# A decoder layer on one core: normalized tokens exchanged through HBM, two buffers for the feed-forward's rows, weights fetched in another order

## The chip, the cores and the metric

The kernel runs on one core of a Trainium2 chip. The metric is the time on the device in microseconds (us), the median of several executions. A profiled execution gives the trace from which all rows below are taken. The engines are TensorE (PE, with its weight loads as PEld), VectorE (DVE), ScalarE (ACT), GpSimd (POOL) and SyncE (SP); a "q" behind an engine's name (SPq) means its instruction queue, here the issuing of DMAs.

## The reference

All numbers are float32. The input `x` is [4, 1024, 512]: four batches of 1024 tokens of 512 features. `_layernorm` has no scale and no shift. Cut to what matters:

```python
def attn(x):              # x is normalized; 16 heads of 32
    aperture, expression = sigmoid(x @ Wa + ba), sigmoid(x @ We + be)   # one number per token and head
    inner, outer, v = x @ Wi, x @ Wo, x @ Wv
    w = softmax(inner @ outer.T / sqrt(32)) * aperture[q] * expression[k]
    w = w / (w.sum(-1) + 1e-8)
    converged = w @ v
    # per head: scale by sigmoid(iv), rotate the two halves of the 32 features, scale by sigmoid(ov), tanh(chi)
    return rotated @ Wout

def xattn(query, key_value):   # key_value is [4, 1024, 384]; 16 heads of 32
    q, k, v = query @ Wq + bq, key_value @ Wk + bk, key_value @ Wv + bv
    return softmax(clip(q @ k.T * 32 ** -0.5)) @ v @ Wo + bo

def ffn(x):                    # 64 units, each with 16 inner values of its own
    s = x @ Win + bin_
    h = relu(s[..., None] * W1 + b1)
    g = einsum('btmh,mh->btm', h, W2) + b2
    return g @ Wout + bout

x = x + attn(_layernorm(x))
x = x + xattn(_layernorm(x), ctx)
x = x + ffn(_layernorm(x))
```

## The kernel before

**Units and halves.** The work is cut in eight units: the gated self-attention of each of the four batches (phase 0, units 0 to 3), then the cross-attention of each (phase 1, units 4 to 7). The feed-forward follows the cross-attention of its tokens. A unit has two halves `hf` of 512 queries. The attention of a half runs over four groups `g` of four heads and, in each, over eight tiles `kt` of 128 keys: 32 steps. In a step, PE computes the scores `s` (L537), ScalarE takes two exponentials `e` of [128, 1024] (L542), VectorE adds them to the running sum `es` (L548, L550; in phase 0 also the gated sum, L558), and one step later PE multiplies `e` by the values into `av` (L564). At the end of a group the sums over partitions are taken with `ones` on PE (L594), they go to HBM and come back as [128, 16] to be inverted, and the reciprocals `rec` return to divide the result (`q`, L644).

**What lies beside the attention.** Everything else is cut into small parts with a cost each, and `run` puts parts between the steps of an attention. The list `beside(u, hf)` gives their order: the projections of the next unit (queries `q`, keys `k`, values `v`, gates `g` and `gt`, layer norm `ln` and transposes `tr`) and the `post` of the half that has just ended (output projection `o`, residual, layer norm, and in phase 1 the feed-forward). What has to be done before the first attention is written out in a list called `first`. `weave` interleaves two lists.

**Order on the engines.** PE, VectorE, ScalarE and GpSimd keep the order in which the program issues instructions (`manual_schedule`). SP and the DMAs are placed by the scheduler; nearly all large DMAs are issued by SP, whose queue is in order: an issue that has to wait for a buffer or for data holds up those behind it.

**Exchange of partitions.** Matmuls need the features on the partitions. `normalized` (L287) writes normalized tokens with tokens on partitions; 32-by-32 blocks are turned by VectorE's `blocks` (L296), and what remains is to exchange blocks between partitions. For the input of an attention, `spread` (L289 to L293) does this with sixteen DMAs of 64 KB from SBUF to SBUF: `xT<-xin`. For the feed-forward, each of four normalized tiles of 128 tokens goes into a tile `r2` (shown as `r` in the profile) of a pool with one buffer, and from there into `rows_d` in HBM (L729, 256 KB each); after the fourth, four DMAs bring it back in the exchanged order into `xn` (L732). The matmul of the feed-forward's first layer is L747.

**The feed-forward's middle.** A half has `s` for two groups of units on 128 partitions. For each of the 16 inner values `h`, ScalarE computes a tile `hid` (L762) from a pool of three buffers, and VectorE adds it, weighted, to `g` (L766, L768). The parts are woven between the steps of the attention. The last matmul of the feed-forward is L779.

**Weights.** `load_w` fetches a weight of 1 MB (or 768 KB) into a pool of three buffers. Four of the weights are fetched by `by_quarters`, L92, in an order of rows that fits the blocks. The weight `Wout` of the self-attention is loaded once (`load_wout`, L151), turned on PE by the heads' rotations (`rotations`, `rotate`), and written to HBM as `wout_d` (L188), from which it is fetched for every use. In the self-attention the weight of the keys is named `Wo`, that of the queries `Wi`.

Of the kernel before, what the change touches and what calls it, by code (L numbers as in the profile page):

```python
# [16 lines left out]
P = 128  # L17
# [22 lines left out]
NB = 32  # L40
# [23 lines left out]
def moderate_path(tc: tile.TileContext, a: dict, out: bass.AP, flag: bass.AP):  # L64
    nc = tc.nc
    x = a["x"]
    with ExitStack() as st:
# [20 lines left out]

        def by_quarters(dma, to, w):

            for q in range(NC):
                dma(to[ts(q, NB)], w[ts(q, P)].rearrange("(c i) f -> i c f", i=NB))  # L92

        x1_d = [[dram.tile([P, D], F32, tag=f"mx1_{b}_{t}", name="x1_d") for t in range(NT)] for b in range(B)]
        x1b_d = [[dram.tile([P, D], F32, tag=f"mxb_{b}_{t}", name="x1b_d") for t in range(NT)] for b in range(B)]
# [2 lines left out]
        sum1_d = [dram.tile([HG, HALF], F32, tag=f"sum1_{i}", name="sum1_d") for i in range(4)]  # L98
        sum2_d = [dram.tile([2, HG, HALF], F32, tag=f"sum2_{i}", name="sum2_d") for i in range(4)]
        rec_d = [dram.tile([HG, HALF], F32, tag=f"rec_{i}", name="rec_d") for i in range(4)]  # L100
        rows_d = [dram.tile([4, P, D], F32, tag=f"rows_{i}", name="rows_d") for i in range(2)]
        wout_d = dram.tile([P, NC, D], F32, name="wout_d")

        ident = const.tile([P, P], F32, name="ident")
# [47 lines left out]
            nc.sync.dma_start(rotj, a["rotj"])  # L152
            nc.sync.dma_start(hp, a["headp"])

        rot = p1.tile([P, NC, P], F32, tag="r2", name="rot")

        def rotations():

# [127 lines left out]
        def normalized(to, xt, mv, rs, i):  # L286
            nc.vector.tensor_scalar(to, xt, mv[:, i, 0:1], rs[:, i : i + 1], ALU.subtract, ALU.mult)  # L287

        def spread(to, xt):  # L289

            for q in range(NC):
                for s in range(P // NB):
                    nc.sync.dma_start(to[ts(q, NB), :, ts(s, P)], xt[ts(s, NB), :, ts(q, P)])  # L293

        def blocks(xt, t):
            nc.vector.transpose(xt[:, t, :], xt[:, t, :])  # L296
# [33 lines left out]
        def pre(u):  # L330
# [29 lines left out]
            def ln(hf):  # L360
                res = {}

                def stats(t):
                    def f():
                        if t == 0:
                            res["mv"] = p2.tile([P, 4, 2], F32, tag="bnmv", name="bnmv")
                        s6 = p2.tile([P, 6], F32, tag="bnst", name="bnst")
                        nc.vector.bn_stats(s6, me["xn", hf][:, t, :])  # L368
                        nc.vector.bn_aggr(res["mv"][:, t, :], s6)
                    return [(0, f)]  # L370

                def root():
                    res["rs"] = rsqrt(res["mv"], 4)

                def norm(t):
                    def f():
                        xt = me["xn", hf][:, t, :]
                        normalized(xt, xt, res["mv"], res["rs"], t)
                        if xt0(hf):
                            return  # L380
                        if t == 3:
                            me["xT", hf] = p2.tile([P, 4, D], F32, tag="inT", name="xT")
                            spread(me["xT", hf], me["xn", hf])
                    return [(0, f)]

                return [stats(t) for t in range(4)] + [[(0, root)]] + [norm(t) for t in range(4)]
# [4 lines left out]
            def tr(hf, t):  # L391
# [8 lines left out]
                    me["in", hf, "t"] = lambda c, i: chunk(xn, c, i, 1)  # L400
                return f

            def proj(what, g, hf):
                kind = "ctx" if ph == 1 and what == "k" else "in"
                n = NCK if kind == "ctx" else NC

                def part(cs):
                    def f():
                        if cs[0] == 0:
                            if g == 0 and hf == 0:  # L410
                                me["w" + what] = load_w(f"{what}{ph}")
                            me["pj"] = bank()
                        for c in cs:
                            columns(
                                me["pj"], me["w" + what][:, c, ts(g, P)], me[kind, hf](c),
                                start=(c == 0), stop=(c == n - 1),
                            )
                        if cs[-1] == n - 1:
                            copy(me["pj"])
                    return len(cs), f  # L420

                def copy(pj):
                    if what == "k":
                        if g == 0 and hf == 0:
                            me["k"] = p2.tile([P, NC, T], F32, tag="k", name="k")
                        dst = me["k"][:, g, ts(hf, HALF)]
                    else:
                        if g == 0:
                            me["q", hf] = p3.tile([P, NC, HALF], F32, tag="q", name="q")
                        dst = me["q", hf][:, g, :]  # L430
                    evacuate(dst, pj, bqk[:, 0 if what == "q" else 1, g : g + 1] if ph else None)

                return [part(list(range(0, 2))), part(list(range(2, n)))]
# [74 lines left out]
                return [[(load, f)]]  # L508

            vs = [values(kt) for kt in range(NT)]  # L510
            r = {"v": [vs[0:4], vs[4:8]]}
            for k, f, load in (
                ("ctx", load_ctx, 0), ("x", load_x, 0), ("g", gates, 1), ("gt", gates_t, 1),
            ):
# [153 lines left out]
        def post(u, hf):  # L668
# [18 lines left out]
            def project(t):  # L687
                def part(cs):
                    def f():
                        assert me["divided", hf] == HG - 1  # L690
                        if cs[0] == 0:
                            res["po"] = bank()
                        for c in cs:
                            columns(
                                res["po"], me["q", hf][:, c, ts(t, P)], me["wo"][:, c, :],
                                start=(c == 0), stop=(c == NC - 1),
                            )
                        if cs[-1] < NC - 1:
                            return
                        r = res[t]  # L700
                        nc.vector.tensor_tensor(r, res["po"], r, ALU.add)  # L701
                        if ph == 0:
                            nc.sync.dma_start(x1_d[b][4 * hf + t], r)
                            r2 = p1.tile([P, D], F32, tag="r2", name="r2")
                            nc.gpsimd.tensor_tensor(r2, r, bo_bc, ALU.add)  # L705
                            nc.sync.dma_start(x1b_d[b][4 * hf + t], r2)
                        else:
                            s6 = p2.tile([P, 6], F32, tag="bnst1", name="bnst1")
                            if t == 0:
                                res["mv"] = p2.tile([P, 4, 2], F32, tag="fmv", name="fmv")  # L710
                            nc.vector.bn_stats(s6, r)
                            nc.vector.bn_aggr(res["mv"][:, t, :], s6)
                    return len(cs), f
                return [part([0, 1]), part([2, 3])]
# [7 lines left out]
            def norm(t):  # L722
                def f():
                    if last:
                        normalized(res["xn"][:, t, :], res[t], res["mv"], res["rs"], t)
                    else:
                        r2 = p1.tile([P, D], F32, tag="r2", name="r2")
                        normalized(r2, res[t], res["mv"], res["rs"], t)
                        nc.sync.dma_start(rows_d[hf][t], r2)  # L729
                        if t == 3:  # L730
                            for q in range(NC):
                                nc.sync.dma_start(  # L732
                                    res["xn"][ts(q, NB)].rearrange("j t (s f) -> j (t s) f", f=P),
                                    rows_d[hf].rearrange("t (s j) f -> j (t s) f", j=NB)[:, :, ts(q, P)],
                                )
                    nc.gpsimd.tensor_tensor(res[t], res[t], bout_bc, ALU.add)
                return [(0, f)]

# [18 lines left out]
            def hidden(h):  # L757
                def f():

                    if h < INNER:  # L760
                        hid = p3.tile([P, 2 * P], F32, tag="hid", name="hid")
                        nc.scalar.activation(  # L762
                            hid, res["s"], AF.Relu, bias=units[:, 1, h : h + 1], scale=units[:, 0, h : h + 1]
                        )
# [72 lines left out]
        def beside(u, hf):  # L837
# [8 lines left out]
            if u + 1 < B:  # L846
                if hf == 0:
                    out = x[1] + k[0][0:1] + p["g"][0] + k[0][1:] + p["gt"][0]
                    if last:
                        out = last["load"] + out + weave(ln[1], last["o"])  # L850
                    else:
                        out = one(rotations) + one(fold_bv) + out + [rotate(c) for c in range(NC)] + ln[1]
                        out += [[(4, fold_bv)]]
                    return out + v[0][0:2] + tr[1] + v[0][2:3] + p["g"][1] + v[0][3:] + p["gt"][1]
                if not next_:
                    return k[1] + last["load"] + v[1] + last["o"] + q[0] + q[1]
# [20 lines left out]
        p = pres[0]  # L877
        first = p["x"][0] + p["ln"][0] + one(negate) + p["tr"][0] + p["k"][0] + p["x"][1] + p["g"][0]
        first += weave(p["ln"][1], p["q"][0]) + p["gt"][0] + p["v"][0][0:3] + p["tr"][1] + p["v"][0][3:] + p["k"][1]
        first += one(load_wout) + pres[1]["x"][0] + p["g"][1] + weave(pres[1]["ln"][0], p["q"][1]) + p["gt"][1]  # L880
        first += p["v"][1][0:3] + pres[1]["tr"][0] + p["v"][1][3:]
        run([lambda: None], first)
        for u in range(n):
            if u == 0:
# [664 lines left out]
```

## Time and profile before

| | us |
|---|---|
| median of three runs | 2363.6 (2359.71 to 2365.66) |
| profiled execution | 2356.22 |
| its span, first to last instruction | 2354.4 |
| PE busy | 2204.8 (94%) |
| VectorE busy | 1558.0 (66%) |
| ScalarE busy | 1231.3 (52%) |
| GpSimd busy | 139.8 (6%) |
| mean granted clock of TensorE | 0.973 |

163.08 MB move in 158343 DMA packets, 69 GB/s in the mean. The page cuts the span in 40 slices of 58.9 us and gives the busy share of each engine in tenths, and the clock that TensorE was granted, in tenths of full speed. Rows of the timeline have the start, the duration, the engine and its line, the operation, "output<-inputs" with shapes, how many instructions were merged, and in brackets how long the engine was idle before and what ended that.

### The profile page before, as it was taken

The page shows a single profiled execution, that of the slowest core. Times are in us where ns is not written, and L with a number is a line of the kernel's source. Part 1 is how long each engine was busy: PE and PEld are TensorE (multiplying, and loading weights), DVE is VectorE, ACT ScalarE, POOL GpSimd, SP SyncE. Part 2 cuts the span into 40 slices and gives each one's busy share as a digit, 9 for nine tenths or more (in the row PEclk, how much of TensorE's full clock was granted, in tenths as well). Part 3 has the DMA queues.
Part 4 walks back from the last instruction along what each step waited for, and adds up shares of the span by engine and source line. Part 5 has one row for each costly group of instructions (what it writes and reads, how often), then busy time and mean ns, then how long its engine had stood idle before and what let it go on. Part 6 is the DMA issues. An engine that isn't in the chain of part 4 may idle for free.

```text
span 2354.4 us, 53085 instructions
## 1 busy us (share of the span) xinstructions
PE 2204.8 (94%) x22610; PEld 555.1 (24%) x22610; DVE 1558.0 (66%) x2485; ACT 1231.3 (52%) x1478; POOL 139.8 (6%) x146
## 2 busy tenths in 40 slices
PE   7897999999999999999999997999899997999974
PEld 2221222222222222222222221222222221222211
DVE  4466666785767765666865677667886777745454
ACT  0053545555455544555556554647465663756551
POOL 3000012000000000000100001010000101010100
PEclk9998999999999999999999998999999998999997
DMA  5403122131321312112421223222322243212020
GB/s 121 131 8 96 31 83 73 36 107 26 101 63 39 93 45 78 51 39 74 117 72 39 83 78 91 74 61 82 104 59 66 78 118 82 65 31 58 29 65 25
DMA packets 158343, 163.08 MB, mean 69 GB/s; under 512 B 50560, under 2 KB 96256, under 8 KB 156944
## 3 DMA queue, kind: packets, MB, share of 16 engines
q1 hardware_dynamic: 154608, 158.55, 23.7%
q8 instruction: 179, 2.93, 0.5%
q0 software_dynamic: 2080, 0.98, 0.3%
q14 instruction: 68, 0.56, 0.1%
q10 hardware_dynamic: 1408, 0.07, 0.0%
HBM read 108.34 MB, written 35.42 MB: 61 GB/s over the span
## 4 chain that ended last, share of the span: by engine, by line
PE 78%; DVE 7%; DMA 7%; SPq 3%; issue 2%; ACT 1%; DVEq 0%; ACTq 0%
PE f L87 30%; PE s L537 21%; PE av L564 17%; PE sm L572 5%; SPq L293 2%; DMA rows_d<-r 2%; PE sm L594 2%; DVE es L550 2%; ACT e L542 1%; DMA xn<-rows_d 1%; PE f L747 1%; PE f L779 1%; DVE r L287 1%; DMA sum_d<-both 1%; DVE bnst L368 0%
## 5 line engine op out<-in xcount | busy, mean ns | idle before, releaser
L542 ACT ACTIVATE e<-s 128x1024 f32<-128x1024 f32 x1024 | 995.0, 1023 | 807.0 <-PE s L537 607.9
L550 DVE TENSOR_TENSOR es<-es,e 128x1024 f32<-128x1024 f32 x528 | 643.4, 1242 | 276.5 <-ACT e L542 275.6
L537 PE MATMUL s<-q,k 32*64 32x512 f32 x8192 | 619.0, 614 | 9.9 <-ACT e L542 8.7
L564 PE MATMUL av<-e,v 128*32 128x512 f32 x4096 | 556.4, 606 | 0.0
L87 PE MATMUL f<-xT,w 128*32 128x512 f32 x2816 | 334.5, 596 | 13.2 <-DMA w<-in_attn_Wo 8.8
L558 DVE SCALAR_TENSOR_TENSOR eg<-e,sw,eg 128x512 f32<-128x512 f32 x448 | 322.3, 754 | 2.3
L87 PE MATMUL f<-w,q 128*32 128x512 f32 x2048 | 246.0, 598 | 10.2 <-DVE q L644 10.2
L537 PEld LDWEIGHTS s<-q,k 32*64 32x64 f32 x8192 | 137.4, 130 | 461.9 <-ACT e L542 247.3
L548 DVE TENSOR_TENSOR es<-e 128x1024 f32<-128x1024 f32 x88 | 108.0, 1247 | 194.8 <-ACT e L542 186.9
L564 PEld LDWEIGHTS av<-e,v 128*32 128x32 f32 x4096 | 88.5, 108 | 405.8 <-issue 402.8
L87 PEld LDWEIGHTS f<-xT,w 128*32 128x32 f32 x2816 | 93.5, 111 | 228.1 <-issue 215.2
L572 PE MATMUL sm<-e,sw 128*2 128x512 f32 x1024 | 135.1, 599 | 0.0
L87 PE MATMUL f<-w,xT 128*32 128x512 f32 x896 | 106.3, 601 | 16.5 <-DMA w<-in_attn_Wv 16.0
L705 POOL TENSOR_TENSOR r<-res,bo_bc 128x512 f32<-128x512 f32 x32 | 46.5, 1452 | 1128.8 <-DVE res L701 1031.9
L594 PE MATMUL sm<-es,ones 128*1 128x512 f32 x352 | 74.0, 620 | 36.7 <-DVE es L550 36.0
L87 PEld LDWEIGHTS f<-w,q 128*32 128x32 f32 x2048 | 67.2, 111 | 166.7 <-issue 150.4
L762 ACT ACTIVATE hid<-sT,units 128x256 f32<-128x256 f32 x128 | 70.7, 612 | 59.9 <-DVE sT L753 58.0
L87 PE MATMUL f<-w,ctxT 128*32 128x512 f32 x768 | 92.8, 592 | 0.0
L87 PE MATMUL f<-ctxT,w 128*32 128x512 f32 x768 | 92.6, 592 | 0.0
L768 DVE SCALAR_TENSOR_TENSOR g<-hid,units,g 128x256 f32<-128x256 f32 x120 | 57.9, 482 | 21.2 <-ACT hid L762 13.3
L701 DVE TENSOR_TENSOR res<-f,res 128x512 f32<-128x512 f32 x64 | 43.9, 685 | 31.3 <-PE f L87 31.3
L644 DVE TENSOR_TENSOR q<-both,recb 128x512 f32<-128x512 f32 x64 | 44.6, 697 | 26.0 <-DMA recb<-rec_d 25.5
(238 smaller groups left out, 1058.2 us busy)
## 6 DMA issues: line engine op xcount, KB each, us to landing
recb<-rec_d SPq DMA_DIRECT2D x256, 64.0 KB
xT<-xin SPq DMA_DIRECT2D x240, 64.0 KB
w<-in_xattn_Wo SPq DMA_DIRECT2D x9, 1024.0 KB
xin<-in_x SPq DMA_DIRECT2D x8, 1024.0 KB
res<-in_x SPq DMA_DIRECT2D x32, 256.0 KB
w<-wout_d SPq DMA_DIRECT2D x8, 1024.0 KB
x_d<-res SPq DMA_DIRECT2D x32, 256.0 KB
x1b_d<-r SPq DMA_DIRECT2D x32, 256.0 KB
```

What stands on the lines that cost most here:

```text
L87: nc.tensor.matmul(to[r], lhsT=lhsT[:, j, :] if len(lhsT.shape) == 3 else lhsT[:, r], rhs=rhs, **flags)
L293: nc.sync.dma_start(to[ts(q, NB), :, ts(s, P)], xt[ts(s, NB), :, ts(q, P)])
L537: nc.tensor.matmul(s[m : m + 64, j, :], lhsT=k[r, g, kt * P + m : kt * P + m + 64], rhs=q[r, g, :], start=True, stop=True,)
L542: nc.scalar.activation(e, s, AF.Exp, scale=SCALE)
L548: nc.vector.tensor_tensor(me["es"][i], me["e", 0][i], es[i], ALU.add)
L550: nc.vector.tensor_tensor(me["es"][i], me["es"][i], es[i], ALU.add)
L558: nc.vector.scalar_tensor_tensor(eg, es[0][:, h, :], gate(kt), eg, ALU.mult, ALU.add)
L564: nc.tensor.matmul(av[r, :], lhsT=me["v"][:, kt, HG * g + h, :], rhs=es[h // 2][:, h % 2, :], start=(kt == 0), stop=(kt == NT - 1),)
L572: nc.tensor.matmul(sm[j * DH : j * DH + sums, :], lhsT=me["sw"][:, t, HG * g + 2 + h, :] if ph == 0 else ones, rhs=me["e", t][1][:, h, :], ...
L594: nc.tensor.matmul(sm[j * DH : j * DH + 1, :], lhsT=ones, rhs=e, start=True, stop=True)
L762: nc.scalar.activation(hid, res["s"], AF.Relu, bias=units[:, 1, h : h + 1], scale=units[:, 0, h : h + 1])
L768: nc.vector.scalar_tensor_tensor(res["g"], res["hid"], units[:, 2, h - 1 : h], res["g"], ALU.mult, ALU.add)
```

## The change

Five things are edited.

1. `spread` is gone. In its place `away` writes two normalized tiles at a time (512 KB) to `rows_d` in HBM, and `back` fetches all four in the exchanged order with four DMAs. The feed-forward uses the same two helpers, one tile at a time as before. `rows_d` is now three tiles taken in turn.
2. `r2` (and the rotations' tile `rot`, which shares its tag) comes from a pool with two buffers instead of one.
3. `hid` comes from a pool with two buffers instead of three.
4. `by_quarters` cuts a weight by the block of columns `c` instead of by the quarter of partitions: each DMA now writes all 128 partitions, one row of 512 numbers in each.
5. The key weight of unit 1 is fetched ahead of its rows and ahead of `Wout` at the end of `first`; a weight is fetched by whichever part needs it first if it is not yet there. In the first half the rotations are moved ahead of the gates and of the remaining key projections.

```diff
         def by_quarters(dma, to, w):
 
-            for q in range(NC):
-                dma(to[ts(q, NB)], w[ts(q, P)].rearrange("(c i) f -> i c f", i=NB))
+            for c in range(NC):
+                dma(to[:, c, :], w.rearrange("(q c i) f -> c q i f", c=NC, i=NB)[c])
...
-        rot = p1.tile([P, NC, P], F32, tag="r2", name="rot")
+        rot = p2.tile([P, NC, P], F32, tag="r2", name="rot")
...
-        def spread(to, xt):
+        turns = [0]
+
+        def away(rows, xt, t, n):
+
+            if t == 0:
+                rows[:] = [dram.tile([4, P, D], F32, tag=f"rows_{turns[0] % 3}", name="rows_d")]
+                turns[0] += 1
+            nc.sync.dma_start(rows[0][t : t + n].rearrange("t p d -> p t d"), xt)
+
+        def back(rows, to):
 
             for q in range(NC):
-                for s in range(P // NB):
-                    nc.sync.dma_start(to[ts(q, NB), :, ts(s, P)], xt[ts(s, NB), :, ts(q, P)])
+                nc.sync.dma_start(
+                    to[ts(q, NB)].rearrange("j t (s f) -> j (t s) f", f=P),
+                    rows[0].rearrange("t (s j) f -> j (t s) f", j=NB)[:, :, ts(q, P)],
+                )
...
+                        if t % 2:
+                            away(res.setdefault("rows", []), me["xn", hf][:, t - 1 : t + 1, :], t - 1, 2)
                         if t == 3:
                             me["xT", hf] = p2.tile([P, 4, D], F32, tag="inT", name="xT")
-                            spread(me["xT", hf], me["xn", hf])
+                            back(res["rows"], me["xT", hf])
...
-                            if g == 0 and hf == 0:
-                                me["w" + what] = load_w(f"{what}{ph}")
+                            if "w" + what not in me:
+                                fetch(what)
...
-                        r2 = p1.tile([P, D], F32, tag="r2", name="r2")
-                        normalized(r2, res[t], res["mv"], res["rs"], t)
-                        nc.sync.dma_start(rows_d[hf][t], r2)
+                        r2 = p2.tile([P, 1, D], F32, tag="r2", name="r2")
+                        normalized(r2[:, 0, :], res[t], res["mv"], res["rs"], t)
+                        away(res.setdefault("rows", []), r2, t, 1)
                         if t == 3:
-                            for q in range(NC):
-                                nc.sync.dma_start(
-                                    res["xn"][ts(q, NB)].rearrange("j t (s f) -> j (t s) f", f=P),
-                                    rows_d[hf].rearrange("t (s j) f -> j (t s) f", j=NB)[:, :, ts(q, P)],
-                                )
+                            back(res["rows"], res["xn"])
...
-                        hid = p3.tile([P, 2 * P], F32, tag="hid", name="hid")
+                        hid = p2.tile([P, 2 * P], F32, tag="hid", name="hid")
...
-                        out = one(rotations) + one(fold_bv) + out + [rotate(c) for c in range(NC)] + ln[1]
-                        out += [[(4, fold_bv)]]
+                        out = one(rotations) + one(fold_bv) + x[1] + k[0][0:1] + [rotate(c) for c in range(NC)]
+                        out += p["g"][0] + k[0][1:2] + [[(4, fold_bv)]] + weave(ln[1], k[0][2:]) + p["gt"][0]
...
-        first += one(load_wout) + pres[1]["x"][0] + p["g"][1] + weave(pres[1]["ln"][0], p["q"][1]) + p["gt"][1]
-        first += p["v"][1][0:3] + pres[1]["tr"][0] + p["v"][1][3:]
+        first += one(lambda: pres[1]["load"]("k")) + pres[1]["x"][0] + p["g"][1] + weave(pres[1]["ln"][0], p["q"][1])
+        first += one(load_wout) + p["gt"][1] + p["v"][1][0:3] + pres[1]["tr"][0] + p["v"][1][3:]
```

More of the change, by code (lines that the diff above doesn't have):

```diff
@@ L100, in moderate_path @@
         rec_d = [dram.tile([HG, HALF], F32, tag=f"rec_{i}", name="rec_d") for i in range(4)]
-        rows_d = [dram.tile([4, P, D], F32, tag=f"rows_{i}", name="rows_d") for i in range(2)]
         wout_d = dram.tile([P, NC, D], F32, name="wout_d")
@@ L401, in tr, with fetch @@
                 return f
+            def fetch(what):
+                me["w" + what] = load_w(f"{what}{ph}")
             def proj(what, g, hf):
@@ L510, in pre @@
             vs = [values(kt) for kt in range(NT)]
-            r = {"v": [vs[0:4], vs[4:8]]}
+            r = {"v": [vs[0:4], vs[4:8]], "load": fetch}
             for k, f, load in (
@@ L703, in f @@
                             nc.sync.dma_start(x1_d[b][4 * hf + t], r)
-                            r2 = p1.tile([P, D], F32, tag="r2", name="r2")
+                            r2 = p2.tile([P, D], F32, tag="r2", name="r2")
                             nc.gpsimd.tensor_tensor(r2, r, bo_bc, ALU.add)
@@ L726, in f @@
                     else:
-                        r2 = p1.tile([P, D], F32, tag="r2", name="r2")
-                        normalized(r2, res[t], res["mv"], res["rs"], t)
-                        nc.sync.dma_start(rows_d[hf][t], r2)
+                        r2 = p2.tile([P, 1, D], F32, tag="r2", name="r2")
+                        normalized(r2[:, 0, :], res[t], res["mv"], res["rs"], t)
+                        away(res.setdefault("rows", []), r2, t, 1)
                         if t == 3:
-                            for q in range(NC):
-                                nc.sync.dma_start(
-                                    res["xn"][ts(q, NB)].rearrange("j t (s f) -> j (t s) f", f=P),
-                                    rows_d[hf].rearrange("t (s j) f -> j (t s) f", j=NB)[:, :, ts(q, P)],
-                                )
+                            back(res["rows"], res["xn"])
                     nc.gpsimd.tensor_tensor(res[t], res[t], bout_bc, ALU.add)
```

## The prediction

> **What bounds the kernel now.** The page comes first: its busy row says TensorE works 2204.8 of the 2354.4 us, VectorE 1558.0, ScalarE 1231.3. The slices show where PE is not full.
>
> ```profile
> PE   7897999999999999999999997999899997999974
> PEclk9998999999999999999999998999999998999997
> ```
>
> So no engine but PE can set the time as a whole, and the change removes no PE work. It can win only PE's gaps and the half-clock stretches behind them. PE's idle stretches between its first and last matmul sum to 125.7 us; PE's waits name their makers.
>
> ```profile
> PE sm L594 <- DVE es L550: 36.0, 6, 12.4
> PE f L747 <- DVE xn L296: 19.0, 7, 5.3
> PE f L87 <- DMA w<-in_attn_Wv: 16.0, 1, 16.0
> PE f L87 <- DMA w<-in_attn_Wo: 8.8, 1, 8.8
> ```
>
> (Columns: total us, times, longest.) These four rows, 79.8 us, all end at something the change touches. The rest (the first transposes 13.6, the tail 4.8 + 10.6 + 10.2) is not touched. The timeline shows what the first row really is: VectorE's `es` is late because VectorE itself stands, in order, in front of a DMA.
>
> ```profile
> 1418.08 11.41 SPq L293 DMA_DIRECT2D xT<-xin  x16
> 1429.59 0.54 SPq L729 DMA_DIRECT2D rows_d<-r  x1
> 1432.10 0.55 DVE L287 TENSOR_SCALAR r<-res,fmv,yi 128x512 f32<-128x512 f32 x1 [3.32 <-DMA rows_d<-r]
> ...
> 1440.07 1.87 PE L594 MATMUL sm<-es,ones 128*1 128x512 f32 x4 [11.78 <-DVE es L550]
> ```
>
> One buffer `r`: the second to fourth normalizations (3.32, 3.03 and 2.11 us) each wait until the row before is in HBM. The first, at 1424.88, could not be written before 1429.59, behind the sixteen issues of `spread`. The prologue on the DMA queue of SP:
>
> ```profile
> 91.26 11.35 SPq L293 DMA_DIRECT2D xT<-xin  x16
> ...
> 107.35 1.88 SPq L92 DMA_DIRECT2D w<-in_attn_Wo  x4
> ...
> 182.88 0.33 SPq L92 DMA_DIRECT2D w<-in_attn_Wv  x1
> 186.55 10.37 SPq L293 DMA_DIRECT2D xT<-xin  x16
> ```
>
> Both weights are issued when they are already needed, and Wv is cut in two by a spread: its last quarter goes out at 204.21.
>
> **The change, part by part.** Instruction order on PE and VectorE stays as it was except in the first half-unit; SP's issues fall from 1286 to 1160.
>
> *Prologue.* The gaps at 108.33 (8.75 us) and 191.37 (15.98). The key weights of unit 1 are now issued before its rows and before Wout, so they go out when a weight buffer comes free (77.8, where Wout went before) and land well before 108. The rotations run earlier, so the folded Wout leaves about 145 to 149 instead of 179.0, and Wv is issued right behind it, all four quarters together, needed at about 185. Both gaps go: 24.7. Behind each, sixteen matmuls took 3.31 and 3.64 us where 1.72 is usual: 3.5 more. Against it I set 3 us: a moved step brings its DMAs (the gate's `iap_d`, the sums) into another order on SP, and the weights load on fewer engines (below). Gain 25.
>
> *Spread becomes two writes of 512 KB and four reads, 15 times.* SP is held about 4 us in place of 10.4 to 11.4, the 2.0 us of a row's landing included (write 1429.59 issued, next norm released 1432.10). The transposes behind it have cover: in units 1 to 3 (330 to 1030 us) PE is fully busy though VectorE stands 6 to 10 us at times. I cost it at nothing there; if the cover failed, a round trip of some 5 us would come up 15 times. The two gaps at 1165 and 1195 (2.6 us, and a half-clock window of 3.4 us behind each, worth half of it) come from a crowded start of the second phase: half of that, 3.
>
> *Two buffers for `r`.* For the three posts at 1428, 1699, 1970 (gaps 11.78, 10.75, 12.44; sum 34.97): SP is free at about 1423, the second norm needs no wait (1429.5), the third waits for write one (about 1432), the fourth follows; `es` and PE start at about 1433.9, not 1440.07. What stays is 5.6 per post: 18 saved. Posts at 1576 and 1846 (gaps at L747, 5.0 and 5.3 with their small parts): the chain of norms ends 4 us earlier, and the rows are there: 9.9, and 3.6 for a half-clock window behind each. Posts at 2112 and 2232 (5.34 + 2.13, 3.98 + 1.55 and a small part; 13.6): partly, since there is less else to do: 8.8, and 2 of clock. The next thing late in each is the transposes of `xn` (0.68 each on VectorE).
>
> Gains: 25 + 3 + 18 + 13.5 + 10.8 = **70 us**.
>
> *`hid` from three buffers to two.* This is the added wait. The rows of ScalarE and of VectorE in a post:
>
> ```profile
> 1459.28 1.94 ACT L542 ACTIVATE e<-s 128x1024 f32<-128x1024 f32 x2 [0.84 <-PE s L537]
> 1461.11 1.09 ACT L762 ACTIVATE hid<-sT,units 128x256 f32<-128x256 f32 x2
> 1462.09 0.68 ACT L266 ACTIVATE q<-f,bqk 128x512 f32<-128x512 f32 x1
> 1462.98 1.94 ACT L542 ACTIVATE e<-s 128x1024 f32<-128x1024 f32 x2 [0.21 <-PE s L537]
> ```
> ```profile
> 1460.34 2.36 DVE L550 TENSOR_TENSOR es<-es,e 128x1024 f32<-128x1024 f32 x2 [0.47 <-ACT e L542]
> 1462.62 1.08 DVE L768 SCALAR_TENSOR_TENSOR g<-hid,units,g 128x256 f32<-128x256 f32 x2
> ```
>
> A step lasts 3.76 us. ScalarE does two `e`, two `hid`, sometimes a copy of `q`; VectorE two `es`, then two `g`. With two buffers `hid` h+1 waits for `g` h-1, which stands behind the step's `es` pair and ends 3.8 us after the first `e` starts; `hid` would start at 2.3. So ScalarE stands 1.5 us, and behind it in order stand the next `e` pair, for which PE's `av` waits, and the copy of `q`. Following the order of the instructions, 5 of the 8 steps of a post do this (four by 1.5, one by 1.03: 7.0). Each of the other three steps gives 0.84 back (ScalarE's idle before `e`), and 1.0 of lag is free since `av` runs a step later: 7.0 - 2.5 - 1.0 = 3.5 per post. Three posts at 1428 to 1970: 10.2; two at 1576 and 1846: 7; the two of the last unit about 2 together; none in the tail, where each `g` follows its `hid` anyway. **19 us**.
>
> **The clock, row against rule.** The Trainium skill, "TensorE: Matmul & The Clock Gate", section "HAM oscillation", warns only of idle gaps over about 3.4 us; by it these stalls of under 1.5 us cost no clock. The trace is stricter (columns: stretch, its us, busy us of PE, PEld, DVE, ACT and POOL, then granted clock, DMA share, GB/s):
>
> ```profile
> 1164.40:1167.80 3.40, 2.38 (x24) 0.57 (x24) 3.40 (x6) 2.02 (x3) 0.00 (x0) 1.00 0.55 166
> 1167.80:1171.20 3.40, 3.40 (x20) 0.77 (x16) 3.40 (x5) 1.75 (x3) 1.78 (x1) 0.50 0.51 105
> ```
>
> A gap of 1.01 us was followed by a window at half clock, which costs 1.7 us. But a gap of 1.36 at 1420.22 was not. By the rule the penalty is 19; by the first row it could be 19 + 35 stalls x 1.7 = 78. A 1.5 us stall of ScalarE mostly reaches PE as under 1 us, so I stand near the rule and add two such windows: 21.
>
> **Weights in another layout.** `by_quarters` now writes all 128 partitions, and its source begins with a dimension of 4 where it began with 32. The nearest rows are the old quarters: `w<-in_attn_Wo`, four of 256 KB, issued 107.35 to 109.2, PE going on at 117.08, so 1 MB in under 10 us. The skill ("DMA: Bandwidth & Descriptors", section "Why a DMA increments its semaphore by 16 and not by 1", "How many engines (k)") says the number of DMA engines divides the outermost dimension of both sides: 4 in place of 16, and this speaks against the change. A 2 KB packet takes 84 ns in this trace; 128 packets on 4 engines are 32 x 0.084 = 2.7 us a quarter, an estimate of 11 us a load if the quarters queue on the same engines, below the landing seen if they don't. Steady loads are issued over 20 us ahead (Wv at 407.8, used 495.5; Wq at 1357.8, used about 1386), so by the row and by the rule alike the cost in the steady part is nothing; only the first loads of the launch can feel it: 1 to 2 us, inside the 3 above. Without cover it would be some 5 us on each of 16 loads; bound from below, a gain of 1 or 2.
>
> **Sum.** -70 + 21 = -49. The profiled execution took 2356.2 us (span 2354.4, 1.8 around it), 7.4 under the median of the runs shown, 2363.6, so those gaps are, if anything, short; I take the difference off the median: about **2314 us**.
>
> **The rivals.**
> - *The `hid` wait costs nothing* (chance 0.12). For: ScalarE idles half of the time. Against: the step's slack is 0.84 us, the stall 1.5. The whole 70: 2285 to 2297.
> - *The wait costs double and brings half-clock windows* (0.20). Penalty 40 to 60, or the gaps of the posts form again at the next wait (the fourth norm, the transposes): 2330 to 2352.
> - *Slower: the clock falls with every `hid` stall* (0.05). Seven posts x five stalls x (1.5 + 1.7) = 112 us, against 70 of gain: 2405. It decides from about 10 us per post on. For: the row at 1165.49. Against: PE has lag to spare, and other gaps of such a size passed at full clock.
> - *No change* (0.03). The gaps at 1428 to 1970 and the prologue are restored by other waits and `hid` eats the rest: within 7 us of 2363.6.
> - *The forecast* (0.60): 2297 to 2330.
>
> A difference of 0.3%, 7 us, is about what a measurement of this kernel can tell from none. Faster 0.92, same 0.03, slower 0.05. The range takes in the cases on both sides but for the ends: 2289 to 2342.
>
> **What the changed profile would show.** PE's waits: no rows for Wo and Wv at L87, `sm <- es` down from 36 to some 17 us, L747 at 5 to 8. SP: no issue group over 5 us at the spread. ScalarE: idle before `hid` L762 behind `g` L768, some 45 us in all, and PE waits for `e` up by about 15. Span near 2305. I am wrong if the `es` gaps stay over 10 us each (then `r` was not their cause), if half-clock windows line the posts, or if PE stands before a weight anywhere after 300 us.

## Result: 1.2% faster, with more than half of the gain given back in two places

The changed kernel takes 2333.45 us (median of four runs, 2330.0 to 2335.63), the kernel before 2361.65 in the same runs. The ratio is 0.9878, 95% interval [0.9857, 0.9898]: 28.8 us less. The forecast was 2314. The two profiled executions lie 23.2 us apart (spans 2331.2 and 2354.4), since that of before lies 5.4 us under its median; where places are compared below, it is between these two.

The page of the changed kernel, the busy row and the slices of PE and its clock:

```profile
PE 2222.9 (95%) x22610; PEld 561.3 (24%) x22610; DVE 1560.7 (67%) x2485; ACT 1234.8 (53%) x1478; POOL 142.5 (6%) x146
PE   5999999999999999999999999999999998999974
PEclk9999999999999999999999999999999999999996
```

The holes of the prologue and the posts are nearly closed, and the clock is better: the time at half clock fell from 127.1 to 82.4 us (some 37 and 24 windows of 3.4 us). Yet the same 22610 matmuls keep PE busy for 18.1 us more than before, and the first slice is emptier (5, was 7). PE's waits (total us, times, longest):

```profile
PE sm L609 <- DVE es L565: 17.0, 7, 5.3
PE f L758 <- DVE xn L306: 15.0, 9, 5.2
...
PE f L313 <- DVE xin L267: 11.8, 1, 11.8
...
PE s L552 <- ACT e L557: 9.5, 20, 1.9
```

The rows for Wv (16.0) and Wo (8.8) are gone, `sm<-es` fell from 36.0 to 17.0. New is a wait of 11.8 us for `xin`, at the very start. A post in the timeline, the one that stood at 1428 before:

```profile
1415.65 0.55 DVE L286 TENSOR_SCALAR r<-res,fmv,yi 128x512 f32<-128x512 f32 x1
1416.23 4.16 SPq L295 DMA_DIRECT2D rows_d<-r  x2
1419.48 0.99 DVE L286 TENSOR_SCALAR r<-res,fmv,yi 128x512 f32<-128x512 f32 x2
1422.34 0.76 DVE L286 TENSOR_SCALAR r<-res,fmv,yi 128x512 f32<-128x512 f32 x1 [1.87 <-DMA rows_d<-r]
1424.28 1.87 PE L609 MATMUL sm<-es,ones 128*1 128x512 f32 x4 [4.96 <-DVE es L565]
```

The write of the first row is issued 0.6 us after its norm begins, no longer 4.7; the second and third norm run one behind the other, and only the last waits, 1.87 us. PE's gap is 4.96 where it was 11.78. This is what the prediction drew (5.6). And the prologue on SP:

```profile
90.12 2.32 SPq L92 DMA_DIRECT2D w<-in_attn_Wo  x4
...
154.59 1.14 SPq L92 DMA_DIRECT2D w<-in_attn_Wv  x2
```

The other half of Wv follows at 157.89. Both weights go out well before the first matmul that reads them: Wo 31 us ahead (120.9), Wv more than 40 (201.1).

To see where the time went, the start of each score matmul (8192 in each trace, in the same order) is set against the same matmul of the kernel before; the difference is PE's lateness. A step in it is a gain (negative) or a loss (positive) at that place. The last column anticipates an experiment: the changed kernel without its two costs.

| place | predicted | changed, lateness step (us) | `e3_hid3_quarters_old` |
|---|---|---|---|
| to the first score | +1 to 2, inside the 25 | +12.3 | -0.7 |
| rest of the first half | -25 in all | -17.5 | -23.5 |
| unit 1, near 375 us | 0 | +2.3 | 0 |
| start of phase 1 | -3 | -4.6 | -6.8 |
| three posts (1428, 1699, 1970) | -18, then +10.2 | -24.2, then +15.3 | -22.5 |
| two posts (1576, 1846) | -13.5, then +7 | -11.6, then +6.7 | -10.3 |
| last unit | -10.8, then +2 | -0.8 | -5.4 |
| behind the last score | 0 | -1.2 | +0.9 |
| sum | -49, two clock windows counted | -23 | -68 |

### The profile page after: what moved, and what is told of

Its sections match the earlier page's. It is cut to its first block, busy times and chain, and to the rows that moved or that the text cites. A ratio compares the mean times of both kernels' runs of the same rounds, so it can differ in the third digit from the quotient of the medians.

```text
span 2331.2 us, 52885 instructions
## 1 busy us (share of the span) xinstructions
PE 2222.9 (95%) x22610; PEld 561.3 (24%) x22610; DVE 1560.7 (67%) x2485; ACT 1234.8 (53%) x1478; POOL 142.5 (6%) x146
## 4 chain that ended last, share of the span: by engine, by line
PE 71%; DVE 12%; DMA 8%; ACT 4%; issue 3%; SPq 1%; ACTq 0%; DVEq 0%; POOL 0%
PE f L87 28%; PE s L552 19%; PE av L579 15%; PE sm L587 5%; DVE es L565 5%; ACT e L557 2%; PE sm L609 2%; DMA xn<-rows_d 2%; DMA rows_d<-r 2%; DMA recb<-rec_d 1%; DMA sum_d<-both 1%; PE f L790 1%; DMA rec_d<-rec 1%; DVE g L779 1%; ACT hid L773 1%
## 5 line engine op out<-in xcount | busy, mean ns | idle before, releaser
L552 PE MATMUL s<-q,k 32*64 32x512 f32 x8192 | 636.9, 614 | 11.0 <-ACT e L557 9.5
L87 PE MATMUL f<-w,q 128*32 128x512 f32 x2048 | 246.3, 598 | 12.1 <-DVE q L659 12.1
L659 DVE TENSOR_TENSOR q<-both,recb 128x512 f32<-128x512 f32 x64 | 45.3, 708 | 39.0 <-DMA recb<-rec_d 38.8
```

The source lines that it names most:

```text
L87: nc.tensor.matmul(to[r], lhsT=lhsT[:, j, :] if len(lhsT.shape) == 3 else lhsT[:, r], rhs=rhs, **flags)
L552: nc.tensor.matmul(s[m : m + 64, j, :], lhsT=k[r, g, kt * P + m : kt * P + m + 64], rhs=q[r, g, :], start=True, stop=True,)
```

## Experiments

Each kernel was timed beside the kernel before; a difference in us is the difference of its ratio from 1 (or of two ratios) times 2361.65. Two such differences compare to about 5 us. Gains and losses by place are again steps of PE's lateness, from one profiled execution of each kernel.

**The layout of the weights.** `e1_quarters_old` is the changed kernel with

```diff
-            for c in range(NC):
-                dma(to[:, c, :], w.rearrange("(q c i) f -> c q i f", c=NC, i=NB)[c])
+            for q in range(NC):
+                dma(to[ts(q, NB)], w[ts(q, P)].rearrange("(c i) f -> i c f", i=NB))
```

> The changed kernel with the old by_quarters (32 partitions to a DMA). Theory: the new layout sends each quarter over few DMA engines; on ScalarE's queue the small loads of wae hold up the eight bias loads behind them (VectorE waits 13.33 us for nbae, PE 11.81 at 16.59 us), so the first score starts 12.3 us later than in the kernel before. With the old layout VectorE waits about 2 us for nbae, the first score starts near 107 and the time falls by 12 us, to 2321. Rival: the bias is late because of other DMAs that SP now issues first; then the wait at nbae stays above 10 us and the time moves by under 3 us.

Measured 2307.8 us, ratio 0.9782 [0.9766, 0.9799]: 51.5 us under the kernel before, 22.7 under the changed one, nearly twice the 12 expected. The first score comes 11.9 us earlier, as the theory said; five more are won in the rest of the first half, 2.3 near 375 and 3.4 at the start of phase 1. The new layout costs in the steady part too. The windows (columns as in the prediction; the last but one is the busy share of 16 DMA engines) of the changed kernel, and then of this one, while the first weights load:

```profile
29.00:33.00 4.00, 3.19 (x64) 2.54 (x60) 1.38 (x2) 0.05 (x1) 0.20 (x1) 1.00 0.31 98
33.00:37.00 4.00, 4.00 (x40) 1.18 (x37) 0.44 (x1) 0.00 (x0) 0.00 (x0) 1.00 0.26 102
```
```profile
17.00:21.00 4.00, 1.97 (x67) 1.70 (x67) 2.77 (x5) 1.28 (x1) 2.63 (x5) 1.00 1.04 286
```

A share of 0.26 to 0.31 is little more than four engines of sixteen at full load, about 100 GB/s, so 1 MB takes 10 us. The packet records agree: from 33 to 37 us four packets were under way for 79% of the time and five for the rest. That is what the rule in the Trainium skill ("DMA: Bandwidth & Descriptors", "How many engines (k)") says, and the estimate of 11 us a load was close. SP is held as well. The issue of the four quarters of Wi, in the kernel before and in the changed one:

```profile
15.02 3.12 SPq L92 DMA_DIRECT2D w<-in_attn_Wi  x4
```
```profile
18.93 9.93 SPq L92 DMA_DIRECT2D w<-in_attn_Wi  x4
```

Wo, the first weight, holds SP about as long in both (9.49 us before, 8.14 after). VectorE's waits in the changed kernel and in `e1_quarters_old` show who suffers:

```profile
DVE q L659 <- DMA recb<-rec_d: 38.8, 15, 8.1
...
DVE nbae L142 <- DMA nbae<-in_attn_be: 13.3, 1, 13.3
```
```profile
DVE q L659 <- DMA recb<-rec_d: 24.1, 16, 4.7
DVE nbae L142 <- DMA nbae<-in_attn_be: 3.3, 1, 3.3
```

Behind these rows are not the weights but small transfers that run beside them: the bias `nbae`, behind which VectorE stands in order, and the reciprocals `recb`. By the packet records the last of the bias moves at 26.7 us, and at 15.8 with the old layout. Near 352 us SP issues `recb` between two quarters of Wo. VectorE's wait for it, in the changed kernel and with the old layout:

```profile
360.72 0.69 DVE L659 TENSOR_TENSOR q<-both,recb 128x512 f32<-128x512 f32 x1 [8.08 <-DMA recb<-rec_d]
```
```profile
337.93 0.69 DVE L659 TENSOR_TENSOR q<-both,recb 128x512 f32<-128x512 f32 x1 [2.14 <-DMA recb<-rec_d]
```

Both ways are slower: from the issue of the write `rec_d` to that of `recb` 7.26 us pass (3.47 with the old layout), from there to VectorE's start 8.27 (6.12). PE, after the slack is used up, comes 2.3 us later. The profile does not say on which engine a packet ran, and SP's own hold is not separated from it; that the small transfers stand behind the weights on the same four engines is the reading that fits, and `e6_wae_old` and `e10_bias_first` test it for the bias.

**Which load delays the bias.** `e6_wae_old` keeps the new layout for the four weights and gives the old one (`by_rows`) to the two loads `wae` on ScalarE's queue.

```diff
-        by_quarters(nc.scalar.dma_start, wae[:, :, 0:H], a["attn_Wa"])
-        by_quarters(nc.scalar.dma_start, wae[:, :, H:], a["attn_We"])
+        by_rows(nc.scalar.dma_start, wae[:, :, 0:H], a["attn_Wa"])
+        by_rows(nc.scalar.dma_start, wae[:, :, H:], a["attn_We"])
```

> The changed kernel with the old order of rows for the two small loads wae alone; the four weights keep the new layout. If the bias is late because of the wae loads ahead of it on ScalarE's queue, VectorE's wait at nbae falls from 13.3 to about 3 us and the time by 12 us. If the loads of the weights Wo, Wi and Wv, which run on the same few DMA engines at that time, hold up the bias, the wait stays above 8 us and the time falls by under 5; the rest of the 22 us that the old layout brought belongs to the weights in either case.

2328.03 us, ratio 0.9862 [0.9848, 0.9876]. The wait at `nbae` stays at 12.3 us, the time falls by 3.8, inside what two such differences can tell. So the loads ahead of the bias on its own queue are not the cause; what is left of the layout is the weights on SP's queue. My first guess in `e1` named the wrong loads.

`e10_bias_first` issues the eight bias loads before `wae`:

```diff
-        by_quarters(nc.scalar.dma_start, wae[:, :, 0:H], a["attn_Wa"])
-        by_quarters(nc.scalar.dma_start, wae[:, :, H:], a["attn_We"])
         nbae = const.tile([P, 1], F32, name="nbae")
         for t in range(4):
...
+        by_quarters(nc.scalar.dma_start, wae[:, :, 0:H], a["attn_Wa"])
+        by_quarters(nc.scalar.dma_start, wae[:, :, H:], a["attn_We"])
```

> The changed kernel with the eight small bias loads issued on ScalarE's queue ahead of the wae loads. Theory: what delays the start is only that the bias loads come up behind the weights on the same DMA engines, and VectorE's negate stands in order before the copies; issued first, they land before 10 us, the wait at nbae goes to 0 and the first score starts 10 to 12 us sooner: -11 us against the changed kernel, to about 2322. Rival: with the bias there, PE waits for Wo instead, which lands late on the four engines (10 us for 1 MB): the start moves by under 4 us.

2322.24 us, ratio 0.9847 [0.9833, 0.9861]: 7.3 us better, where the theory had 11. The wait at `nbae` is gone, but the first score comes only 3.6 us sooner, as the rival had it: PE now waits elsewhere, and for a weight.

```profile
PE f L87 <- DVE xT L306: 4.3, 1, 4.3
PE f L87 <- DMA w<-in_attn_Wo: 3.8, 1, 3.8
```

Yet by the end of the first half PE is 9.1 us ahead of the changed kernel, out of the 16.9 that the old layout wins there. So the place of the bias is about half of what the layout costs in the prologue. Wo, late behind it, is a part of the other half; the rest was not traced to single transfers.

**The layout alone.** `e9_before_quarters_new` is the kernel before with the new `by_quarters` and nothing else.

> The kernel before with only the new by_quarters. Theory: four DMA engines to a quarter, so the first loads take 10 us each one after the other and the bias lands 10 us late: the first score starts 11 to 12 us later than at 107.2; the two weights that are late in the prologue come later still (some 3 to 6 us more before Wo and Wv), the steady loads stay hidden except where they crowd other transfers (2 to 3 us near 380 and 1190): +17 to +24 us against the kernel before, to about 2380. Rival: the new layout hurts only together with the exchange through HBM, whose transfers it shares the engines with; alone it costs under 8 us.

2371.32 us, ratio 1.0058 [1.0044, 1.0073]: 13.7 slower, under the 17 to 24 expected. The first score comes 11.7 later; but the gaps before the matmuls that read Wo and Wv shrink (5.91 from 8.75, 12.19 from 15.98), they don't grow, as I had it. (The profile puts the 5.91 down to `rot`, which these matmuls don't read; after eight of them PE stands another 0.27 for Wo.) Why they shrink is open. A later start of PE is no reason for Wo: SP issues it 1.0 us before PE needs it in both kernels. By the end of the first half 7.1 us of the loss are left, three more come near 375, and 3.4 at the start of phase 1. VectorE's waits for `recb` are 46.4 us, 25.5 in the kernel before. The rival falls: the layout costs by itself.

**The feed-forward's buffers.** `e2_hid3` gives `hid` three buffers again (SBUF is full, so the gates' tile takes its place in the same pool):

```diff
-                    gi = p2.tile([P, P], F32, tag="gi", name="gi")
+                    gi = p3.tile([P, 2 * P], F32, tag="hid", name="gi")[:, 0:P]
...
-                        hid = p2.tile([P, 2 * P], F32, tag="hid", name="hid")
+                        hid = p3.tile([P, 2 * P], F32, tag="hid", name="hid")
```

> The changed kernel with three buffers for hid again (the room comes from the gates' tile gi, which now takes its place in the same pool). Theory: ScalarE's waits for g (35.4 us, 30 times) go to below 5, and the lateness that PE gathers in the posts (4.1 us in each of three, 3.4 in each of two, 2 to 3 in each of the last two) goes: about -22 us, to 2311. Rival: the posts are bound by the next thing in line anyway (PE's slack, VectorE's order), and the time falls by under 8.

2305.38 us, ratio 0.9778 [0.9765, 0.9792]: 23.6 us better than the changed kernel. The waits of `hid` for `g` go from 35.4 us (30 times) to 0.3. In the changed kernel the wait looks like this on ScalarE, and beside it on PE:

```profile
1449.56 1.92 ACT L557 ACTIVATE e<-s 128x1024 f32<-128x1024 f32 x2
1451.37 0.60 ACT L773 ACTIVATE hid<-sT,units 128x256 f32<-128x256 f32 x1
1453.45 0.60 ACT L773 ACTIVATE hid<-sT,units 128x256 f32<-128x256 f32 x1 [1.48 <-DVE g L779]
1453.96 1.92 ACT L557 ACTIVATE e<-s 128x1024 f32<-128x1024 f32 x2
```
```profile
1450.62 2.00 PE L552 MATMUL s<-q,k 32*64 32x512 f32 x16
```

and on PE with three buffers:

```profile
1448.00 1.11 PE L552 MATMUL s<-q,k 32*64 32x512 f32 x16
```

The second `hid` stands 1.48 us (1.5 predicted) and the step grows from 3.76 to 4.40 us. On PE hardly an idle stretch appears: the sixteen score matmuls take 2.00 us in place of 1.11, because they wait for the PSUM tiles that the late `e` still read. The first eight start at 1450.62, just after the first `e` has ended (1450.57), the other eight at 1451.54, just after the second (1451.48). The wait hides inside PE's busy time. That is where the 18.1 us come from by which the busy row rose; with three buffers it is 2200.2. By place, PE loses 15.3 us behind the gaps of the three posts in the changed kernel and 1.1 in this one. No window at half clock lies among the stalls beside the posts: the windows there begin at 1421, 1688, 1954, 2101 and 2220 and last 6.8 us, and the stalls of the first post, for one, run from 1447 to 1472.

**Both undone.** `e3_hid3_quarters_old` has both edits.

> Both edits of the two kernels before this one. If the two costs lie at different places, as the theory has it, they add up: -34 us, to about 2299. If they cover each other, the time is that of the better one alone.

2288.27 us, ratio 0.9702 [0.9688, 0.9716]: 70.4 us under the kernel before, 41.6 under the changed one. The two costs (22.7 + 23.6 = 46.3) add up within the 5 us that two differences can tell. This version beats both kernels.

**The rows' second buffer.** `e5_rows_one` puts `r2` and `rot`, three places with one tag, back to one buffer in the changed kernel. One of the three:

```diff
-                        r2 = p2.tile([P, 1, D], F32, tag="r2", name="r2")
+                        r2 = p1.tile([P, 1, D], F32, tag="r2", name="r2")
```

> The changed kernel with one buffer for the feed-forward's normalized tiles (and the other tiles of that tag) again. Theory: the single buffer makes each norm wait for the write before it (3 waits of 2 to 3.3 us in each of seven posts); the three gaps at sm<-es go from 5.2 to about 10, those at L758 grow by 2 to 4: +22 us over the changed kernel, some 6 us under the kernel before. Rival: what was won in those gaps was the 4.2 us that the first write stood behind the sixteen issues of spread; then one buffer costs under 8 us.

2349.62 us, ratio 0.996 [0.9946, 0.9973]: 19 us slower than the changed kernel, so the theory (22) holds. VectorE's waits for the write of a row:

```profile
DVE r L286 <- DMA rows_d<-r: 40.1, 20, 3.5
```

They are 11.9 us with two buffers and were 49.9 in the kernel before. The gaps at `sm<-es` are 8.1, 7.9 and 8.0: between the 5 of two buffers and the 10 expected, so about 3 us of each came from the single buffer and some 4 from the rest. (`e4_rows_one`, with a single buffer for `r2` beside two for the other tiles of its tag, gave no time: its pools do not fit in SBUF.)

**The exchange through HBM.** `e8_spread_back` is `e3_hid3_quarters_old` with the sixteen SBUF-to-SBUF DMAs of `spread` for the attention's input.

```diff
-                        if t % 2:
-                            away(res.setdefault("rows", []), me["xn", hf][:, t - 1 : t + 1, :], t - 1, 2)
...
-                            back(res["rows"], me["xT", hf])
+                            spread(me["xT", hf], me["xn", hf])
```

> The changed kernel with old by_quarters and three hid buffers, and the sixteen SBUF-to-SBUF DMAs of spread again in place of away and back for the attention's input (the feed-forward keeps away and back, with two buffers). Theory: SP is held 10 to 11 us per spread; the first write of the feed-forward's rows stands behind it, the gaps at sm<-es grow from 5 to about 9, Wv is late in the prologue: +15 to +20 us over the same kernel with the exchange through HBM, some 50 under the kernel before. Rival: with two row buffers and weights issued early nothing waits for SP: within 5 us.

2313.97 us, ratio 0.9805 [0.9793, 0.9818]: 24.3 us slower than with the exchange through HBM, more than the 15 to 20 expected. The gaps at `sm<-es` grow to 7.1, 6.7 and 7.3, less than expected; 12.1 us are lost in the prologue, 6.3 at the start of phase 1 and 8.5 in the posts. Wv is not late in it. What is late shows best in the next kernel.

**The order alone.** `e7_before_order` is the kernel before with the prologue's order, and old exchange, layout and buffers.

```diff
...
-        first += one(load_wout) + pres[1]["x"][0] + p["g"][1] + weave(pres[1]["ln"][0], p["q"][1]) + p["gt"][1]
-        first += p["v"][1][0:3] + pres[1]["tr"][0] + p["v"][1][3:]
+        first += one(lambda: pres[1]["load"]("k")) + pres[1]["x"][0] + p["g"][1] + weave(pres[1]["ln"][0], p["q"][1])
+        first += one(load_wout) + p["gt"][1] + p["v"][1][0:3] + pres[1]["tr"][0] + p["v"][1][3:]
```

> The kernel before with only the fetching order and the rotations' place taken from the change; spread, by_quarters, hid and r as before. Theory: the two gaps before Wo (8.75) and Wv (15.98) close with their half-clock matmuls: -22 to -25 us against the kernel before, the second half onward unchanged. Rival: the spread's sixteen issues still stand ahead of Wv or Wo on SP, and one of the gaps comes back: -5 to -12.

2347.51 us, ratio 0.9947 [0.9934, 0.996]: 12.5 us faster, half of the theory's figure, the upper end of the rival's. Both waits for weights are gone; in the place of the one for Wv stands another. SP, VectorE and ScalarE of this kernel:

```profile
178.91 11.43 SPq L293 DMA_DIRECT2D xT<-xin  x16
...
192.78 0.67 SPq L609 DMA_DIRECT2D cs<-sum_d  x1
```
```profile
198.16 0.19 DVE L621 TENSOR_TENSOR both__1658<-cs 128x32 f32<-128x32 f32 x1 [11.85 <-DMA cs<-sum_d]
```
```profile
201.83 1.94 ACT L545 ACTIVATE e<-s 128x1024 f32<-128x1024 f32 x2 [8.71 <-DVE eg L561]
```

The spread holds SP for 11.4 us; the sums of a head group get out to HBM and back only behind it, VectorE waits 11.85 us for them in order, frees no `e`, ScalarE stands 8.71 and PE 6.96. In the kernel before the same wait (9.81 us on VectorE, ended at 202.9) lay hidden under PE's wait for Wv. So in the prologue the order is worth 12 us alone and 24 with the exchange through HBM. The exchange without the order was not tried.

## Why the prediction was right, and what was mis-sized

The direction, the added wait and the range came out; the time lies 19 us above the 2314 of the sum. By its number it falls in the stretch of the rival "the wait costs double" (2330 to 2352) and not in that of the forecast (2297 to 2330). But the rival's mechanism is not what happened: the `hid` wait cost 23.6 us, not 40 to 60, and brought no half-clock windows. Another term carried the time there.

- **The gains, 70 us: right.** Without the two costs the kernel is 70.4 us faster. By place the terms are within 6 us each: prologue 24.2 (25), phase start 6.8 (3), three posts 22.5 (18), two posts 10.3 (13.5), last unit 5.4 (10.8). That the sum fits to 1 us is luck: two terms were 8.3 too small, three 9.4 too large. In the last unit the norm chain is 2.4 us shorter in each post, and that is the gain; I had worked it as the gap less 2.4, though the way of the last row to HBM and back stays (the transposes wait 5.31 us, 5.36 before).
- **The `hid` wait, 21 us: right.** 23.6 by time. The stalls (1.48), their number (30 of the 35 worked out) and the steps' slack came out as worked. By place it was larger in the three posts (15.3, worked out 10.2) and as worked in the two (6.7 and 7). How it shows on PE did not come out: I expected PE's wait for `e` to grow by 15 us; it grew by 0.8, and the loss sits in busy time.
- **The clock.** No half-clock window lies among the `hid` stalls beside the posts, so the term near the rule of the Trainium skill ("TensorE: Matmul & The Clock Gate", "HAM oscillation": only idle gaps over about 3.4 us) held and the harsher reading of the row at 1165.49 did not, and the slower rival, a clock that falls with every stall, had no ground. What decides about gaps between the two is open: 1.01 us at 1165.49 was followed by such a window in the kernel before, 1.51 and 1.18 us on PE at 1568 and 1834 in the changed kernel were not.
- **The mis-sized term: "weights in another layout", 1 to 2 us, inside the 3 set against the prologue.** It measured 22.7 in the changed kernel, 13.7 alone in the old one. The rule was read rightly and its 10 us a load are seen. What failed was the step from there to "the cost in the steady part is nothing": I looked at when each weight is needed and not at what else moves while it loads. "PE stands before a weight after 300 us" was the wrong alarm; it did not go off, and VectorE stood before small transfers instead (`nbae` 13.3 us, 3.3 with the old layout; `recb` 38.8, 24.1).
- The rest of the profile's forecasts: `sm<-es` at 17 (17.0 measured), no weight rows: right. The idle time of `hid` behind `g` some 45 us (35.4): near. L758 at 5 to 8 (15.0): wrong, 10.1 of it in the last unit. SP's issues were also miscounted: the traces have 1229 and 1079, not 1286 and 1160.

## What to carry to other kernels

Ask of a transfer not only when it must be there but which engines it fills and for how long; a load that is itself well ahead can delay a bias of a few bytes that an in-order engine is waiting for. A buffer given to one tile and taken from another is two edits: here each was worth about 20 us, with opposite signs, and one small tile moved into the same pool paid for both. A wait removed from in front of PE can uncover another that ended at nearly the same time: with the order alone the prologue won 12 us, with the exchange as well 24.

## What the runs showed of the hardware that I had not expected

- Four quarters of 256 KB whose source begins with a dimension of 4 keep the DMA share at 0.26 to 0.31 and move about 100 GB/s; with 32 in front the share was 1.04 and 286 GB/s, in a window that other transfers share. SP's issue of the four of Wi took 9.93 us against 3.12, that of the first weight, Wo, 8.14 against 9.49.
- Loads on ScalarE's queue (the bias) were delayed by those on SP's queue: 13.3 us of wait against 3.3, and 12.3 with the old layout on ScalarE's own queue alone.
- PE's busy time takes in stalls inside a group of matmuls: 2.00 us for sixteen that need 1.11.
